# Graph attention on one core: bias of V by VectorE for six tiles of eight, one sum with x moved to GpSimd, one slot's weighing moved to ScalarE, and a new order of work

## The chip, the cores and the metric

The kernel runs on one core of a Trainium2 chip. The metric is the time on the device in microseconds (us), and less is better. The core has TensorE (PE, matrix products into PSUM), VectorE (DVE), ScalarE (ACT), GpSimd (POOL, which here also issues the indirect DMAs), and SyncE (SP, which issues the plain DMAs). Each engine works through its own list of instructions in order. Where one waits, all that stand behind it on that engine wait too.

## The reference

```python
# x (16, 1024, 512), adj (1024, 1024) of zeros and ones, Wq, Wk, Wv (512, 512), 8 heads of 64
h = max(layernorm(x), 0)
q, k, v = h @ Wq + bq, h @ Wk + bk, h @ Wv + bv      # split into heads
scores = q k^T / 8, and -1e9 where adj is 0
out = x + softmax(scores) v                          # per batch, heads side by side
```

The graph is the same for all 16 batches, and each row has few neighbours (the longest lists belong to a few rows).

## The kernel before

**Beginning, once.** The kernel counts each row's neighbours (`degree`), ranks the rows by that number, and lists each row's neighbours (`list_of`). The ranks and the layer norm's factors of batch 0 go through a table in DRAM (`tell`, then `collect`), the lists go through another (`spread`, `collect`). What comes back is a permutation of the rows (`perm_of`) and an index for each gather (`spots`). The rows with the longest lists have what exceeds 11 neighbours cut into pieces of four (`long_rows`, `long_blocks`, `longest`, `count_pieces`, `first_piece`, `owners`, `flip_owners`, `copy_owners`, `list_pieces`, `pieces`, `slots`).

**Each batch.** A batch has eight tiles of 128 rows, in the order 7, 6, 5, 4, 3, 2, 1, 0, so the place `n % 8` of a tile in its batch is 0 for tile 7 and 7 for tile 0. Tile t holds rows with at most `CAPS[t]` neighbours. Per tile:

- `load_x` (GpSimd's indirect DMA), `stats`, `variance`, `power`, `shift` for the layer norm, and `norm` on ScalarE.
- `flip`: four transposes by TensorE; `unflip`: ScalarE copies the result out of PSUM.
- `proj_kv`: K and V, each four fp32 matmuls of 128x512 into one of two PSUM buffers (`pkv`). The bias is a bf16 matmul of 128x512 more (line 1055), or it is left out there and VectorE adds a row of biases while it copies V out of PSUM (line 1073). `bias_by` decides by the table `BIAS_V`. Without it ScalarE copies K or V out (line 1075). This is `evict_kv`; `store_kv` writes both to DRAM.
- `queries`: the same for q, always with the bias by TensorE, into one of two PSUM buffers.

The neighbours' rows of K and V are then fetched in 14 units per batch (`gather`, up to four slots each, six SBUF buffers `g`). Per unit VectorE forms the scores (`multiply`, line 1298; `score`, line 1302), ScalarE the exponent, and each slot's V is weighed: by VectorE in one instruction per slot (`weigh_v`, line 1318), or by ScalarE in eight, one per head (`weigh_s`, line 1332). `by_vector` says how many slots of a unit VectorE takes: `BY_VECTOR` by the unit's size, and one more for the units in `ONE_MORE`. Slots are added (`fold`, line 1337; `join`, line 1344); for tile 0 TensorE does part of that (`add_up`, line 1356; `pass_on` carries a sum of pieces, line 1371). `scale` divides by the sum of weights, `residual` adds x (line 1406; `residual_by_vector` chooses VectorE or GpSimd), `put_out` writes the tile.

K and V of batch b + 1 are projected while batch b's neighbours are weighed. K and V of batch 0 come from the rows as they stand, before the ranking is known (`first` in the names).

**What sets the order.** Every operation has a place, a number in `PLACES`, by batch (the once-only work, `first`, 0, 1, 2, 3 for all in the middle, `next` for the last but one, `last`). `Plan.ordered` sorts each engine's operations by place, and takes at each step the one with the lowest place whose producers and buffers are given. The places are sort keys that were found by a search, not times. The order comes out fixed, engine by engine.

Of the kernel before, what the change touches and what calls it, by code (L numbers as in the profile page):

```python
# [57 lines left out]
UNITS = tuple(unit for t in TILES for unit in PARTS[t])  # L58
# [14 lines left out]
ONE_MORE = ((2, 0),)  # L73
LAST_BY_VECTOR = {(2, 0): 0, (2, 3): 0, (0, 0): 0, (-1, 0): 0, (3, 0): 0, (1, 4): 0}
VECTOR_RESIDUAL = (4,)
# [22 lines left out]
        list_of=(-13.2, -13.4, 13.93, 14.05, -4.33, -7.76, -9.88, 14.25,),  # L98
        tell=(-12.63, -16.97, -13.14, 9.24, 0.89, 16.11, 17.75, 19.88,),
        spread=(45.38, 47.45, 30.7, 45.48, 45.35, 30.46, 22.54, 45.26,),  # L100
        collect=(-9.17, 5.02,),
        others=(14.42,),
        perm_of=(0.42,),
        spots=(26.84,),
        long_rows=(30.4,),
        long_blocks=(16.58, 20.59, 22.61, 24.22, 24.98,),
        longest=(27.18, 29.37, 32.28, 35.43, 36.11, 39.52, 41.52, 44.79, 45.14,),
        count_pieces=(46.89,),
        first_piece=(122.72,),
        owners=(94.07,),  # L110
        flip_owners=(136.43,),
        copy_owners=(113.68,),
        list_pieces=(137.27,),
        pieces=(127.38,),
        slots=(142.24,),
        add_bias=(-19.2, -17.6,),
        spread_bias=(68.07,),
        copy_bias=(89.7,),
# [4 lines left out]
        norm=(75.49, 76.09, 77.09, 77.49, 79.89, 80.09, 80.34, 80.69,),  # L123
        flip=(75.49, 75.69, 76.49, 76.69, 78.69, 78.89, 90.39, 104.64,),
        unflip=(75.89, 76.49, 77.29, 77.89, 80.49, 80.72, 96.22, 97.88,),
        proj_kv=(75.89, 77.49, 76.29, 77.89, 76.89, 78.49, 79.09, 79.29, 86.87, 98.15, 99.79, 107.75, 135.06, 147.6, 153,
            148.32,),
        evict_kv=(76.89, 79.29, 77.69, 79.49, 78.09, 80.29, 80.4, 80.66, 96.1, 96.13, 96.42, 106.28, 154.55, 162.49, 169.71,
            172.46,),
        store_kv=(78.35, 116.17, 119.38, 125.35, 140.7, 146.55, 148.18, 147.06,),  # L130
        variance=(75.89, 76.89, 79.29, 81.69,),
        power=(75.69, 76.29, 78.29, 87.8,),
# [3 lines left out]
        load_x=(30.09, 30.5, 38.8, 45.21, 45.44, 47.92, 49.07, 49.69,),  # L136
        norm=(2.13, 2.31, 24.77, 49.09, 71.39, 77.14, 77.27, 78.66,),
        flip=(50.32, 51.95, 54.11, 55.9, 60.64, 67.45, 67.52, 68.48,),
        unflip=(27.69, 53.06, 72.64, 77.2, 79.54, 81.13, 82.77, 84.23,),
        queries=(67.49, 69.07, 115.56, 126.07, 127.49, 138.29, 148.67, 168.76, 169.97,),  # L140
        gather=(45.09, 65.92, 63.96, 81.66, 82.98, 67.8, 87.05, 86.63, 69.01, 87.14, 102.98, 103.26, 67.61, 108.86, 109.63,
            108.64, 107.92, 79.49, 116.69, 119.1, 130.36, 131.45, 130.44, 102.76, 142.21, 138.67, 142.4, 144.98, 150.63,
            142.37, 142.46, 108, 152.91, 152.09, 152.7, 153.37, 153.1, 152.82, 153.23, 171.08, 171.84, 155.19, 172.79,
            155.41, 171.17, 171.11,),
        multiply=(47.46, 64.59, 81.01, 107.03, 126.74, 113.33, 126.77, 141.63, 149.43, 155.18, 163.45, 170.22, 180.88,
            178.07,),
        score=(47.54, 67.41, 96.06, 111.76, 129.2, 117.87, 128.06, 146.83, 153.31, 155.84, 165.66, 174.39, 181.78, 195.93,),
        exponent=(92.19, 93.82, 105.44, 111.15, 115.51, 115.42, 115.56, 141.97, 143.4, 152.67, 166.31, 172.53, 173.27,
            183.23,),
        row_sums=(64.37, 70.18, 97.04, 118.27, 142.77, 160.52, 163.48, 203.64,),  # L150
        share=(64.49, 74.75, 101.56, 119.16,),
        weigh_v=(69.44, 130.54, 142.01, 144.6, 161.03, 163.57, 170.25, 175.36, 195.82,),
        weigh_s=(92.85, 101.83, 100.44, 95.75, 106.78, 112.94, 106.75, 115.48, 115.39, 115.45, 122.29, 116.89, 121.19, 119.7,
            142.94, 135.53, 142.97, 143.03, 144.58, 154.99, 152.31, 153.27, 163.13, 166.52, 165.91, 171.8, 172.93, 171.74,
            173.08, 173.04, 172.99, 174.92, 175.62, 181.86, 185.22, 185.42, 187.44,),
        fold=(71.91, 97.01, 97.07, 132.47, 137.68, 138.95, 141.69, 143.23, 145.64, 143.05, 153.79, 155.15, 156.82, 161,
            163.76, 171.2, 173.85, 175.66, 181.17, 186.5, 187.92, 183.84, 200, 202.21, 204.35, 204.53,),
        residual=(109.25, 124.53, 138.45, 141.77, 153.19, 171.14, 178.55, 219.35,),
        put_out=(129.95, 130.51, 141.35, 142.43, 153.4, 178.16, 179.5, 225.23,),
        join=(147.89, 161.06, 175.01,),  # L160
        scale=(148.16, 161.67, 176.53, 211.41,),
        copy_q=(145.23,),
        add_up=(188.54, 194.88, 203.87, 205.55,),
        more=(201.41,),
        pass_on=(203.77,),
        seen=(331.72,),
    ),
    1: dict(
        load_x=(-45.57, -43.85, -39.73, -39.1, -35.32, -8.38, 7.1, 14.11,),
        stats=(-63.36, -61.71, -54.75, -49.26, -50.34, -20.16, 1.69, 45.35,),  # L170
        norm=(-12.29, -8.07, -1.29, 11.92, 17.92, 21.28, 45.19, 45.66,),
        flip=(-14.6, 13.76, 33.62, 50.55, 65.56, 72.21, 73.87, 79.53,),
        unflip=(-6.21, -2.22, 15.4, 21.31, 28.65, 37.54, 57.61, 68.73,),
        proj_kv=(17.02, 20.04, 31.75, 42.81, 49.67, 52.6, 71.12, 55.79, 72.24, 74.1, 74.46, 79.5, 79.61, 83.24, 86.3, 90.4,),
        evict_kv=(-2.01, -35.87, 14.8, 20.07, 20.47, 37.41, 38.89, 36.39, 47.71, 60.13, 57.69, 63.79, 70.59, 76.3, 77.5,
            77.55,),
        store_kv=(7.84, 6.03, 7.72, 17.75, 21.65, 22.37, 41.88, 46.5,),
        variance=(-59.83, -48.24, 0.42, 46.54,),
        power=(-31.44, 7.33, 34.59, 50.93,),
        shift=(-56.77, -25.47, 22.23, 52.69,),  # L180
        queries=(92.98, 95.46, 99.76, 113.88, 114.01, 119.61, 134.23, 135.77, 151.42,),
        gather=(53.63, 85.6, 64.02, 85.49, 85.7, 72.03, 102.18, 95.44, 87.81, 104.49, 108.17, 108.68, 107.7, 109.8, 109.4,
            111.58, 112.73, 107.63, 119.79, 126.28, 135.9, 135.96, 135.93, 140.28, 147.73, 148, 149.33, 149.5, 150.8, 150.83,
            149.71, 142.94, 156.83, 157.14, 151.75, 157.7, 150.86, 150.89, 162.73, 165.24, 165.07, 165.98, 165.43, 166.72,
            176.54, 166.09,),
        multiply=(100.67, 106.6, 119.91, 124.46, 149.54, 145.64, 149.6, 154.01, 164.31, 168.95, 171.4, 175.59, 182.84,
            188.66,),
        score=(107.36, 108.32, 124.43, 142.56, 149.57, 145.7, 153.22, 157.27, 165.13, 170.5, 171.68, 182.66, 188.41, 193.53,),
        exponent=(101.25, 100.12, 106.42, 110.23, 116.2, 116.09, 136.58, 137.26, 142.79, 164.86, 172.22, 183.82, 187.9,
            189.8,),  # L190
        row_sums=(111.52, 118.48, 124.49, 145.67, 151.53, 163.54, 171.43, 223.45,),
        share=(112.04, 119.71, 124.55, 145.84,),
        weigh_v=(115.89, 145.87, 155.15, 158.81, 169.44, 171.46, 193.56, 188.61, 193.59,),
        weigh_s=(102.16, 107.3, 103.87, 104.01, 107.98, 108.93, 112.16, 116.05, 121.06, 115.46, 125.94, 135.88, 136.78,
            122.78, 137.3, 139.07, 140.95, 141.59, 137.36, 163.59, 164.34, 153.33, 167.75, 166.89, 171.97, 181.76, 182.84,
            176.37, 187.96, 186.35, 188.1, 189.16, 190.92, 190.49, 191.49, 191.11, 190.86,),
        fold=(119.37, 124.52, 136.3, 135.99, 136.05, 152.83, 147.47, 157.39, 160.24, 157.34, 165.19, 168.14, 169.06, 169.41,
            174.3, 178.51, 174.7, 177.42, 193.62, 193.65, 193.68, 198.47, 195.72, 204.29, 208.27, 212.87,),
        residual=(113.65, 130, 143.43, 153.45, 160.4, 179.56, 185.95, 209.42,),
        put_out=(129.97, 136.02, 156.67, 157.96, 166.22, 183.18, 187.67, 215.86,),  # L200
        join=(163.89, 169.49, 187.98,),
        scale=(164.12, 171.36, 188.49, 227.3,),
        copy_q=(144.08,),
        add_up=(188.22, 192.32, 197.88, 215.67,),
        more=(188.38,),
        pass_on=(191.08,),
        seen=(236.64,),
    ),
    2: dict(
        load_x=(-56.28, -51.47, -39.61, -36, -12.07, 6.83, 6.86, 40.79,),  # L210
# [499 lines left out]
def by_vector(b, B, u):  # L710

    count = UNITS[u][2]
    if b == B - 1:
        return LAST_BY_VECTOR.get(UNITS[u][:2], 1)
# [893 lines left out]
```

## Time and profile before

| | us |
|---|---|
| median of 3 runs (lowest, highest) | 1613.55 (1610.17, 1617.66) |
| the profiled execution: its own time | 1612.02 |
| its span, first to last instruction | 1609.9 |
| PE busy / DVE / ACT / POOL | 1572.1 / 1518.2 / 1444.8 / 1258.7 |
| mean granted TensorE clock | 0.992 of full |
| moved by DMA | 531.56 MB, mean 330 GB/s |

What lies around the span is 1612.02 - 1609.9 = 2.1 us. A busy time is a sum over instructions as the profile shows them; neighbouring instructions overlap a little, so the step from one start to the next is shorter than the duration shown.

### The profile page before, as it was taken

The numbers are of one execution on the slowest core, as the hardware profiler recorded it, in microseconds if no ns is written. First come the engines' busy times: TensorE is split into PE (matmuls) and PEld (weight loads), VectorE is DVE, ScalarE is ACT, GpSimd is POOL, SyncE is SP. The second block draws the span as 40 slices with busy tenths as digits, with TensorE's granted clock in tenths as the row PEclk, the third lists the DMA queues.
The fourth block names the chain that finished last, engine by engine and source line by source line (L and its number), as shares of the span: only waits on it lengthen the run. The fifth ranks groups of instructions, "written<-read, shape, count | busy, mean of one in ns | idle before, by whom it ended". The sixth has DMA issues, their size and how long they took to land. (4 is left out here: it accounts for less than half of the span.)

```text
span 1609.9 us, 19515 instructions
## 1 busy us (share of the span) xinstructions
PE 1572.1 (98%) x4242; PEld 732.0 (45%) x4242; DVE 1518.2 (94%) x2075; ACT 1444.8 (90%) x5428; POOL 1258.7 (78%) x1185
## 2 busy tenths in 40 slices
PE   8999999999999999999999999999999999999687
PEld 4444444444444444444444444444444444444233
DVE  8889999999999999999999999999999999999897
ACT  4459999898999989899898989999998998989897
POOL 3777778887788888888788787878788887786666
PEclk9999999999999999999999999999999999999899
DMA  6499989999999999999999999999999999998886
GB/s 249 141 351 341 334 319 358 329 366 323 341 333 345 366 333 357 325 351 349 339 357 346 345 337 345 344 343 352 330 339 331 341 373 326 338 335 330 324 306 217
DMA packets 149876, 531.56 MB, mean 330 GB/s; under 512 B 19052, under 2 KB 19052, under 8 KB 149752
## 3 DMA queue, kind: packets, MB, share of 16 engines
q0 software_dynamic: 109840, 390.70, 67.9%
q1 hardware_dynamic: 39912, 139.56, 23.0%
q8 instruction: 35, 0.57, 0.1%
q14 instruction: 89, 0.73, 0.1%
HBM read 429.46 MB, written 100.72 MB: 329 GB/s over the span
## 5 line engine op out<-in xcount | busy, mean ns | idle before, releaser
L1332 ACT ACTIVATE g<-g,weights 128x64 f32<-128x64 f32 x4704 | 1160.3, 338 | 40.9 <-DVE weights L1311 37.8
L1288 POOL DMA_INDIRECT g<-kv,index x608 | 642.2, 1056 | 206.7 <-issue 163.2
L1057 PE MATMUL pq<-wq,hT 128*128 128x512 f32 x1024 | 462.4, 595 | 0.0
L1057 PE MATMUL pk<-wk,hT 128*128 128x512 f32 x960 | 431.7, 593 | 0.0
L1057 PE MATMUL pv<-wv,hT 128*128 128x512 f32 x960 | 431.4, 593 | 0.0
L1302 DVE TENSOR_REDUCE weights<-g 128x32 f32<-128x2048 f32 (+2 forms) x224 | 423.7, 1897 | 2.0
L1298 DVE TENSOR_TENSOR g<-g,pq 128x2048 f32<-128x2048 f32 (+2 forms) x208 | 388.7, 1870 | 28.1 <-DMA g<-kv 9.9
L1057 PEld LDWEIGHTS pq<-wq,hT 128*128 128x128 f32 x1024 | 195.8, 191 | 216.9 <-issue 213.2
L1057 PEld LDWEIGHTS pv<-wv,hT 128*128 128x128 f32 x960 | 182.4, 190 | 213.5 <-issue 210.6
L1057 PEld LDWEIGHTS pk<-wk,hT 128*128 128x128 f32 x960 | 182.7, 190 | 201.4 <-issue 196.8
L1337 DVE TENSOR_TENSOR g<-g 128x512 f32<-128x512 f32 (+1 forms) x301 | 253.9, 851 | 9.8 <-ACT g L1332 8.4
L1409 POOL DMA_INDIRECT out_dram<-x,perm x128 | 136.7, 1068 | 39.8 <-issue 30.6
L1002 POOL DMA_INDIRECT x<-in_x_dram,perm x128 | 135.8, 1061 | 34.9 <-issue 32.5
L1337 POOL TENSOR_TENSOR g<-g 128x512 f32<-128x512 f32 x90 | 115.0, 1284 | 17.6 <-DVE g L1337 10.5
L1037 ACT ACTIVATE h<-x,shift,rstd 128x512 f32<-128x512 f32 x120 | 96.5, 807 | 12.0 <-DVE shift L1027 11.4
L1318 DVE TENSOR_TENSOR g<-g,weights 128x512 f32<-128x512 f32 x143 | 101.9, 716 | 1.1 <-ACT weights L1306 0.6
L1356 PE MATMUL acc<-g,ident 128*128 128x512 f32 x170 | 84.4, 612 | 14.6 <-ACT g L1332 10.8
L1044 PEld LDWEIGHTS pht<-ident,h 128*128 128x128 f32 x512 | 63.2, 141 | 68.6 <-issue 52.7
L1406 POOL TENSOR_TENSOR x<-x,o 128x512 f32<-128x512 f32 x64 | 81.9, 1280 | 9.4 <-DVE o L1392 5.0
L1049 ACT COPY hT<-pht 128x512 f32<-128x512 f32 x128 | 73.0, 571 | 16.3 <-PE pht L1044 16.2
L1011 DVE BATCH_NORM_STATS2 st<-x 128x6 f32<-128x512 f32 x120 | 81.2, 677 | 1.6 <-DMA x<-in_x_dram,perm 1.6
L1044 PE MATMUL pht<-ident,h 128*128 128x128 f32 x512 | 76.5, 273 | 3.2 <-ACT hT L1049 1.9
(242 smaller groups left out, 1080.2 us busy)
## 6 DMA issues: line engine op xcount, KB each, us to landing
g<-kv SPq DMA_DIRECT2D x128, 512.0 KB, 7.7
kv<-kvt SPq DMA_DIRECT2D x120, 512.0 KB, 6.9
g<-kv,index POOLq DMA_INDIRECT x608, 6.9
adj<-in_adj_dram SPq DMA_DIRECT2D x8, 512.0 KB, 8.2
x_first<-in_x_dram SPq DMA_DIRECT2D x8, 256.0 KB, 6.0
x<-in_x_dram,perm POOLq DMA_INDIRECT x128, 5.5
out_dram<-x,perm POOLq DMA_INDIRECT x128, 6.6
wk<-in_L_gnn_Wk_dram SPq DMA_DIRECT2D x1, 1024.0 KB
```

What stands on the lines that cost most here:

```text
L1002: nc.gpsimd.indirect_dma_start(out=X[n][:], out_offset=None, in_=x_rows, in_offset=on(ap=perm[:, t : t + 1], axis=0), element_offset=b * N * D
L1037: nc.scalar.activation(HN[n], X[n], AF.Relu, bias=shift, scale=scale)
L1044: nc.tensor.transpose(PH[n][:, c, :], hn[:, ts(c, P)], ident)
L1057: nc.tensor.matmul(pt, HT[n][:, c, :], W[name][:, c, :], start=(apart and c == 0), stop=(n != -NT and c == DC - 1))
L1288: nc.gpsimd.indirect_dma_start(out=G[i][:, s].rearrange("p j d -> p (j d)"), out_offset=None, in_=KV[b % len(KV)][:], in_offset=on(ap=inde ...
L1298: nc.vector.tensor_tensor(k, k, Q[b, t][:, None, :].to_broadcast([P, count, D]), ALU.mult)
L1302: nc.vector.tensor_reduce(weights[:, w, :], heads(G[i][:, :count, 0, :]), AX.X, ALU.add)
L1318: nc.vector.tensor_tensor(v, v, own.to_broadcast([P, n, H, HD]), ALU.mult)
L1332: nc.scalar.activation(v[:, h, :], v[:, h, :], AF.Identity, scale=weights[:, c + s, h : h + 1])
L1337: engine.tensor_tensor(v[:, 0:n], v[:, 0:n], v[:, first : first + n], ALU.add)
L1356: nc.tensor.matmul(ACC[b, home], owner_t if t < 0 else ident, v[:, s, :], start=(u == added_up(b, B, home)[0] and s == 0), stop=(u == adde ...
L1409: nc.gpsimd.indirect_dma_start(out=out_rows[t], out_offset=on(ap=perm[:, t : t + 1], axis=0), in_=X.pop(b * NT + TILES.index(t))[:], in_of ...
```

## The change

The tables that say which engine does what:

```diff
-ONE_MORE = ((2, 0),)
+ONE_MORE = ()
 LAST_BY_VECTOR = {(2, 0): 0, (2, 3): 0, (0, 0): 0, (-1, 0): 0, (3, 0): 0, (1, 4): 0}
-VECTOR_RESIDUAL = (4,)
+NEXT_BY_VECTOR = {}
+VECTOR_RESIDUAL = ()
+NEXT_VECTOR_RESIDUAL = ()
...
-BIAS_V = {0: 'DVE', 2: 'DVE', 4: 'DVE', 6: 'DVE'}
+BIAS_V = {0: 'DVE', 1: 'DVE', 2: 'DVE', 3: 'DVE', 4: 'DVE', 6: 'DVE'}
+LAST_BIAS_V = BIAS_V
...
 def residual_by_vector(b, B, t):
-    return t in (VECTOR_RESIDUAL if b < B - 1 else LAST_VECTOR_RESIDUAL)
+    return t in (LAST_VECTOR_RESIDUAL if b == B - 1 else NEXT_VECTOR_RESIDUAL if b == B - 2 else VECTOR_RESIDUAL)
...
-def bias_by(n, name):
+def bias_by(n, name, B):
+    kinds = LAST_BIAS_V if n >= (B - 1) * NT else BIAS_V
+    return kinds.get(n % NT, "PE") if n >= 0 and name == "v" else "PE"
```

So in each of the 15 batches whose K and V are projected from ranked rows (1 to 15), the tiles at places 1 and 3 lose the bias matmul of V, and their V leaves PSUM through VectorE's addition in place of ScalarE's copy. In batches 0 to 14 the sum of tile 4 with x goes from VectorE to GpSimd, and one slot of the first unit of tile 2, `(2, 0)`, goes from VectorE's one instruction to ScalarE's eight. The last batch's weighing and sums stay as they were.

Every place in `PLACES` from `list_of` on is replaced. Three parts of it, cut to what is spoken of below:

```diff
-        list_of=(-13.2, -13.4, 13.93, 14.05, -4.33, -7.76, -9.88, 14.25,),
+        list_of=(-13.2, -13.4, -4.81, -4.72, -4.29, -5.81, -11.81, -10.72,),
...
-        count_pieces=(46.89,),
-        first_piece=(122.72,),
+        count_pieces=(56.74,),
+        first_piece=(75.94,),
...
-        copy_owners=(113.68,),
+        copy_owners=(170.86,),
...
-        norm=(2.13, 2.31, 24.77, 49.09, 71.39, 77.14, 77.27, 78.66,),
+        norm=(10.32, 13.57, 14.06, 23.48, 49.11, 49.2, 52.33, 56.26,),
```

In the order that comes out, the list of each engine keeps its operations apart from those moved. In the beginning GpSimd stores two tiles of K and V ahead of all the `tell`s, where before it stored one behind the first of them; ScalarE does the norms of batch 0's tiles at places 4 and 5 ahead of the last eviction of `first` K and V, where before the second of them stood behind it; on VectorE `count_pieces` stands behind the first `multiply`, and on TensorE `first_piece` ahead of the queries of tile 5, where before it was the other way round in both. At the end, all engines keep the same operations behind the last projection of K and V, with neighbours swapped here and there.

## The prediction

> **What bounds the kernel now.** I read the page's busy times first, then the slices, then each engine's windows and waits in the middle, then the list of TensorE's instructions in time.
>
> ```profile
> PE 1572.1 (98%) x4242; PEld 732.0 (45%) x4242; DVE 1518.2 (94%) x2075; ACT 1444.8 (90%) x5428; POOL 1258.7 (78%) x1185
> ...
> PE   8999999999999999999999999999999999999687
> ...
> PEclk9999999999999999999999999999999999999899
> ```
>
> TensorE is busy in all slices but the first and the last few. A busy PE need not be PE at its peak, so its windows and its list must confirm it.
>
> ```profile
> 300.00:900.00 600.00, 599.88 (x1621) 280.00 (x1620) 577.71 (x747) 565.09 (x2153) 490.11 (x450) 1.00 0.95 344
> ```
>
> The columns are the window, its length, then busy time of PE, PEld, DVE, ACT and POOL, the granted clock, the DMA share and GB/s. PE is without a gap for 600 us at full clock. Its list shows what a bias costs there:
>
> ```profile
> 827.93 3.60 PE L1057 MATMUL pv<-wv,hT 128*128 128x512 f32 x8
> 831.37 0.60 PE L1044 MATMUL pht<-ident,h 128*128 128x128 f32 x4
> ...
> 835.45 0.38 PE L1055 MATMUL pv<-bias_parts,chosen 128*128 128x512 bf16 x1
> 835.67 3.60 PE L1057 MATMUL pv<-wv,hT 128*128 128x512 f32 x8
> ```
>
> From start to start a projection takes 831.37 - 827.93 = 3.44 us and its bias 0.22 (0.216 over many pairs), though the bias is shown as 0.38. A batch's 24 projections (3.43 each), 20 biases, 8 flips (0.435), 4 additions and one product with the pieces (0.86 each) and `pass_on` (0.14) sum to 94.6 us. The starts of `pass_on` in the list are 94.64 apart (468.77, 563.42, 658.06). So in the middle the time is TensorE's work and nothing else.
>
> At the end it is not. The last projection ends near 1503.5; the last batch's gathers, scores and weighing follow, and TensorE mostly waits:
>
> ```profile
> 1512.91 2.05 PE L1356 MATMUL acc<-g,ident 128*128 128x512 f32 x2 [9.20 <-ACT g L1332]
> ```
>
> **The change, part by part.** The rows by shape (count | busy, mean ns | idle before):
>
> ```profile
> L1332 ACT ACTIVATE g<-g,weights 128x64 f32<-128x64 f32 x4704 | 1160.3, 338 | 40.9 <-DVE weights L1311 37.8 <-DMA g<-kv,index 0.4 <-issue 0.2
> ...
> L1318 DVE TENSOR_TENSOR g<-g,weights 128x512 f32<-128x512 f32 x143 | 101.9, 716 | 1.1 <-ACT weights L1306 0.6
> ...
> L1406 POOL TENSOR_TENSOR x<-x,g 128x512 f32<-128x512 f32 x45 | 58.0, 1289 | 4.7 <-ACT h L1037 1.6 <-issue 1.6
> ...
> L1073 DVE TENSOR_TENSOR kvt<-pv,bias_rows 128x512 f32<-128x512 f32 x60 | 41.0, 683 | 5.2 <-PE pv L1057 5.1
> ...
> L1075 ACT COPY kvt<-pv 128x512 f32<-128x512 f32 x60 | 34.4, 573 | 7.3 <-PE pv L1057 7.0
> ...
> L1055 PE MATMUL pv<-bias_parts,chosen 128*128 128x512 bf16 x60 | 22.8, 379 | 0.0
> ...
> L1406 DVE TENSOR_TENSOR x<-x,g 128x512 f32<-128x512 f32 x16 | 10.7, 666 | 0.0
> ```
>
> *TensorE.* Two biases fewer in each of 15 batches: 30 x 0.216 = 6.5 us, all on the path, so a period of 94.64 - 0.43 = 94.2.
>
> *VectorE.* By steps from start to start: two evictions of V more (0.60 each), one `weigh_v` less (0.60), one sum less (0.58), so 0.02 us more per batch. Nothing in itself, but the period shrinks by 0.43 around it. Its waits over eight periods (468.77 to 1226.15):
>
> ```profile
> DVE g L1298 <- DMA g<-kv: 8.6, 8, 1.7
> DVE g L1298 <- PE pq L1057: 3.2, 5, 0.6
> ...
> DVE g L1298 <- DMA g<-kv,index: 2.0, 2, 1.9
> ```
>
> All its waits there are 22.7 us, 2.84 per batch, of which 0.99 are for TensorE and so real slack; 1.85 are for gathers, ScalarE and GpSimd. Work and contention make 94.67 - 2.84 + 0.02 + 0.05 = 91.90 us (the 0.05 is worked out under GpSimd), which leaves 94.20 - 91.90 = 2.30 for waits that need 1.85. It still fits, barely. I charge 1.0 us in all for places where it doesn't, bounds 0 and 6 (TensorE losing all that it gained).
>
> Behind each new eviction on VectorE stand sums of weights, folds and the next `multiply`, and the next projection but one waits for its PSUM buffer. Summing TensorE's work in the changed order between the end of a projection and the one that reuses its buffer gives 11.4 us of cover for place 1 and 7.3 for place 3. The five VectorE operations ahead of each sum to 6.0 and 5.5 us by their steps, so even with all of them still to do both are covered. The evictions at places 4 and 6, on VectorE already, have 4.1 and 3.65 us (4.9 and 4.1 before). Without cover each costs what it is late.
>
> *ScalarE.* Two copies less (0.47 from start to start), eight heads of one slot more (1.92): 0.98 per batch. Its waits in the same eight periods are 40 us, 5 per batch, so about 3.6 remain: hidden. The first fold of that unit waits for ScalarE's third slot instead of a `weigh_v`; the new order puts it behind the `multiply` and `score` of the first unit of tile 1, where before it stood ahead of both.
>
> *GpSimd.* One sum more, 1.28 per batch at 82% busy, hidden. It follows GpSimd's own last fold of that tile, so it waits for nothing new. Behind it stand three gathers of the second unit of tile 1, each issued in 0.94; `multiply` on VectorE waits for them, and if they come late it is by this 1.28 (the bound of 6 holds a part of that in each batch).
>
> A GpSimd sum and a VectorE sum can hinder each other:
>
> ```profile
> 1499.60 1.29 POOL L1337 TENSOR_TENSOR g<-g 128x512 f32<-128x512 f32 x1
> ```
>
> ```profile
> 1500.01 1.97 DVE L1337 TENSOR_TENSOR g<-g 128x1024 f32<-128x1024 f32 x1
> ```
>
> The same fold takes 1.22 at 854.71; here it lasts until just past its rival, 0.75 longer. Most escape: the means of `weigh_v` (716 against a median of 683) and of the folds (some 15 and 45 above the usual) make about 11 us over the run, against 199 GpSimd sums, so 0.05 each. The Trainium skill, "SBUF — State Buffer", section "Who interferes with whom", speaks against this move: two instructions that both read through the pair of ports that VectorE and GpSimd share don't share time, the second stops until the first ends. By that at its worst VectorE would lose 1.28 us per batch, and the 1.0 us charged above would be 6. I go by the rows.
>
> *Beginning.* The order of TensorE is the same to 60.2 us. Then, before:
>
> ```profile
> 76.56 0.60 PE L1044 MATMUL pht<-ident,h 128*128 128x128 f32 x4
> 79.08 0.66 PE L1044 MATMUL pht<-ident,h 128*128 128x128 f32 x4 [1.91 <-ACT hT L1049]
> ...
> 79.89 5.19 PE L1057 MATMUL pq<-wq,hT 128*128 128x512 f32 x8
> ```
>
> and the window of the same 4 us:
>
> ```profile
> 80.00:84.00 4.00, 4.00 (x7) 1.62 (x6) 3.72 (x14) 1.59 (x3) 3.08 (x4) 0.61 0.88 322
> ```
>
> ScalarE had a norm behind the last eviction of the first K; TensorE waited 1.91 us, the clock fell to 0.61, and a projection took 5.19 for 3.60: with the slower bias 1.75 us lost. Waits of 1.39 (at 10 and 19.7 us) cost no clock. The new order puts that norm ahead of the eviction; the next flip then still waits for an eviction, an unflip and a norm, some 0.9 us. Lead: 1.0, and 1.75 with the clock kept.
>
> Against it, `first_piece` now stands ahead of the third tile's queries and needs `count_pieces`, which stands behind the first `multiply`. That `multiply` began at 96.45, 9.3 us after its first gather was issued (87.15). GpSimd has the same operations ahead of this gather in both orders; three of them took about 0.95 longer than the usual 0.95 before (43.67, 50.96, 55.70), so it is issued between 85.0 and 87.2. TensorE would reach `first_piece` at 97.9 - 2.8 = 95.1 and get it 1.9 us after the `multiply` begins, between 96.2 and 98.4. The lead of 2.8 shrinks by 1.1 to 3.3, and 1.75 more is lost if the clock falls. Another stall of 0.7 us (at 102, for the second `multiply`) falls away, as the queries that met it come later. So between 2.4 us gained and 1.6 lost; I take 1.0 gained, the middle of the two issue times (1.3) less some risk of the clock.
>
> *End.* Both orders have the same ten `weigh_s` on ScalarE and the same additions on VectorE behind the last eviction; GpSimd starts the last batch's gathers when the last `store_kv` has landed. The end moves forward as a whole: 0, bounds 2 gained and 3 lost, by VectorE's waits there (6 us in the last 78).
>
> **Sum.** 1612.0 - 6.5 - 1.0 + 1.0 = 1605.5 for a profiled execution; the profiled one lay 1.5 under the median, so 1607. Its own range is 1603 to 1611.
>
> **Rivals.**
> - *VectorE becomes the bound (slower).* Place: its waits for gathers in each middle batch. Point: waits not for TensorE above 2.30 us per batch. One more late gather per batch like the longest shown (1.9) makes 1.85 + 1.9 = 3.75, a period of 91.90 + 3.75 = 95.65, 1.45 above 94.2, 21.8 over 15 batches in place of the 1.0: 1606 + 21.8 = 1628. For it: DMA is 95% busy, and every place is new. Against: TensorE has no waits in the middle now, and others wait for it.
> - *The gain is mostly eaten.* Those waits come to 2.3 to 2.7, so 0.3 us per batch: 1611 to 1616, no change to be told.
> - *More than the biases.* The beginning gains 2.4, the end 2, and VectorE's term is 0: 1607 - 1.4 - 2 - 1.0 = 1602.6; 1600 to 1603 with a little more at the end.
> - That the change doesn't do what it says is excluded by the order: 30 bias matmuls fewer, 30 VectorE evictions more.
>
> **Numbers.** My forecast 0.60, VectorE as the bound 0.17, mostly eaten 0.18, more gained 0.05. A measurement of this kernel can tell about 0.5%, 8.07 us, from no change: faster is below 1605.5. A little under half of the forecast's chance lies there: 0.29 + 0.05 = 0.34. The rest, 0.31 + 0.18 = 0.49, is the same; slower is 0.17. The range 1600 to 1622 leaves out the slow case and a little of the best.
>
> **What would show it.** Right: `pass_on` starts 94.2 apart, PE without idle from 110 us to the last projection, which ends near 1497; L1055 for pv x30, L1073 x90, L1332 x4824. Right in the beginning: no clock below 1.00 near 80 us, a stall of 1 to 3 us near 95. Wrong: periods above 94.3 with PE waiting for `pkv` or `q` buffers, VectorE's waits for gathers above 2.3 us per batch, or more than 106 us from the last projection to the end.

## The result, and the profile after

The changed kernel takes 1661.29 us (median of 5 runs, 1658.95 to 1661.64) against 1616.53 for the kernel before (5 runs): a ratio of 1.0281, 95% interval 1.0262 to 1.0300. It is 44.8 us slower, and 54 above the forecast of 1607. The profiled execution has a span of 1659.5, 49.6 more than before.

The page first: TensorE's share fell from 98% to 95%.

```profile
PE 1583.9 (95%) x4180; PEld 731.8 (44%) x4212; DVE 1520.8 (92%) x2075; ACT 1463.3 (88%) x5518; POOL 1266.3 (76%) x1200
...
PE   8999999999999999999999999999999999999687
...
PEclk9999999999999999999999999999999999999889
```

The slices look as they did before: a loss of 3% in every slice is still a 9. The windows show it (window, length, busy time of PE, PEld, DVE, ACT, POOL, clock, DMA share, GB/s):

```profile
300.00:900.00 600.00, 582.83 (x1536) 269.54 (x1546) 557.59 (x723) 551.58 (x2101) 471.81 (x441) 0.99 0.91 332
900.00:1000.00 100.00, 97.19 (x255) 44.73 (x257) 91.43 (x118) 91.52 (x351) 75.56 (x73) 0.98 0.91 330
```

Before, PE had 599.88 of these 600 us. Now every engine has less, and the clock is below 1. The starts of `pass_on` are 98.96 apart (784.53, 883.50, 982.46), not 94.20. The waits, over the whole run, name one line (total, times, longest):

```profile
PE pv L1060 <- ACT kvt L1078: 28.1, 11, 3.1
```

Ten of these eleven are one in each of batches 3 to 12, always at the same point. TensorE's list there (start, duration):

```profile
942.57 3.60 PE L1060 MATMUL pv<-wv,hT 128*128 128x512 f32 x8
...
950.53 1.02 PE L1278 MATMUL pq_-1_8022<-q,owner 128*128 128x512 f32 x2
954.25 5.40 PE L1060 MATMUL pv<-wv,hT 128*128 128x512 f32 x8 [2.70 <-ACT kvt L1078]
959.49 0.38 PE L1058 MATMUL pk<-bias_parts,chosen 128*128 128x512 bf16 x1
```

The V projected at 942.57 is that of place 5, which ScalarE copies out; the V at 954.25 is that of place 6 and wants the same PSUM buffer. It starts 2.70 us late, and then takes 5.40 in place of 3.60. Why ScalarE is late stands in ScalarE's list:

```profile
943.80 2.02 ACT L1335 ACTIVATE g<-g,weights 128x64 f32<-128x64 f32 x8
949.04 0.59 ACT L1282 COPY q<-pq 128x512 f32<-128x512 f32 x1 [3.22 <-DVE g L1301]
949.52 2.03 ACT L1335 ACTIVATE g<-g,weights 128x64 f32<-128x64 f32 x8
951.45 0.22 ACT L1309 ACTIVATE weights<-weights 128x32 f32<-128x32 f32 x1
951.70 2.03 ACT L1335 ACTIVATE g<-g,weights 128x64 f32<-128x64 f32 x8
953.63 0.56 ACT L1078 COPY kvt<-pv 128x512 f32<-128x512 f32 x1
```

L1282 is `copy_q`, which copies the queries of tile 0 out of PSUM. It waits 3.22 us for VectorE's first `multiply` of tile 0. In the profile before, `copy_q` (L1279) has no such wait:

```profile
713.97 0.59 ACT L1279 COPY q<-pq 128x512 f32<-128x512 f32 x1
```

VectorE's list of the changed kernel at that point:

```profile
946.73 2.28 DVE L1301 TENSOR_TENSOR g<-g,pq 128x2048 f32<-128x2048 f32 x1
951.58 1.23 DVE L1340 TENSOR_TENSOR g<-g 128x1024 f32<-128x1024 f32 x1 [2.58 <-ACT g L1335]
```

`copy_q` and that `multiply` only read `pq`, so the data ask for no order between them. The built program has a wait between them all the same, in either order (no run here leaves it out): of these two readers of a PSUM tile on two engines, the one written down later waits for the one written down earlier. The instruction of batch 6 in the two builds, before and after (`PE_49` counts TensorE's work, `DVE_49` VectorE's):

```
L1279 TensorCopy q0_6_6153<-pq_6_0_6147 128x512 [waits PE_49]
L1282 TensorCopy q0_6_6300<-pq_6_0_6140 128x512 [waits DVE_49]
```

In the order of before, `copy_q` was written down 7 to 61 operations ahead of that `multiply` (one ahead in batch 15), so it was the `multiply` that had to come behind the copy, which was long done. In the new order `copy_q` comes five operations behind the `multiply` in batches 3 to 12 (and two in 15), and the wait turned round. VectorE then waits in turn for ScalarE's weighing (the 2.58 at 951.58).

The rows that the forecast spoke of, by shape (count | busy, mean ns | idle before):

```profile
L1335 ACT ACTIVATE g<-g,weights 128x64 f32<-128x64 f32 x4824 | 1198.9, 346 | 20.9 <-DVE weights L1314 16.8 <-issue 2.4
...
L1321 DVE TENSOR_TENSOR g<-g,weights 128x512 f32<-128x512 f32 x128 | 99.5, 779 | 0.2 <-ACT weights L1309 0.2
...
L1409 POOL TENSOR_TENSOR x<-x,g 128x512 f32<-128x512 f32 x60 | 76.7, 1279 | 6.8 <-ACT h L1040 2.8 <-issue 1.0 <-DVE g L1340 0.2
...
L1076 DVE TENSOR_TENSOR kvt<-pv,bias_rows 128x512 f32<-128x512 f32 x90 | 61.4, 683 | 21.6 <-PE pv L1060 21.6
...
L1058 PE MATMUL pv<-bias_parts,chosen 128*128 128x512 bf16 x30 | 11.4, 379 | 0.5 <-DVE kvt L1076 0.5
```

The change did what it says. `weigh_v` (L1321) has a mean of 779 ns where it had 716.

The sum of the two spans: 30 biases less, -6.5; nine periods from 487.64 to 1378.86 take 891.2 where 9 x 94.20 would be 847.8, +43.4, less the 1.3 by which before's own nine exceed 9 x 94.64; a tenth wait, at 461.13, +2.8; seven waits between 119 and 304 us of 7.5 in all where before had one of 0.2, +7.3; from the last projection of K and V to the end 107.8 in place of 106.2, +1.6. That is 47.3 of the 49.6.

### The profile page after: what moved, and what is told of

It is laid out like the page before. It is cut to its first block, busy times and chain, and to the rows that moved or that the text cites. A ratio compares the mean times of both kernels' runs of the same rounds, so it can differ in the third digit from the quotient of the medians.

```text
span 1659.5 us, 19557 instructions
## 1 busy us (share of the span) xinstructions
PE 1583.9 (95%) x4180; PEld 731.8 (44%) x4212; DVE 1520.8 (92%) x2075; ACT 1463.3 (88%) x5518; POOL 1266.3 (76%) x1200
## 5 line engine op out<-in xcount | busy, mean ns | idle before, releaser
L1335 ACT ACTIVATE g<-g,weights 128x64 f32<-128x64 f32 x4824 | 1198.9, 346 | 20.9 <-DVE weights L1314 16.8
L1291 POOL DMA_INDIRECT g<-kv,index x608 | 627.9, 1033 | 226.1 <-issue 145.5
L1060 PE MATMUL pv<-wv,hT 128*128 128x512 f32 x960 | 447.9, 611 | 28.1 <-ACT kvt L1078 28.1
L1301 DVE TENSOR_TENSOR g<-g,pq 128x1536 f32<-128x1536 f32 (+2 forms) x208 | 388.3, 1868 | 24.4 <-DMA g<-kv,index 9.9
L1005 POOL DMA_INDIRECT x<-in_x_dram,perm x128 | 137.1, 1071 | 37.5 <-issue 35.7
L1321 DVE TENSOR_TENSOR g<-g,weights 128x512 f32<-128x512 f32 x128 | 99.5, 779 | 0.2 <-ACT weights L1309 0.2
L1409 POOL TENSOR_TENSOR x<-x,g 128x512 f32<-128x512 f32 x60 | 76.7, 1279 | 6.8 <-ACT h L1040 2.8
```

The costliest lines, as they stand in the source:

```text
L1005: nc.gpsimd.indirect_dma_start(out=X[n][:], out_offset=None, in_=x_rows, in_offset=on(ap=perm[:, t : t + 1], axis=0), element_offset=b * N * D
L1060: nc.tensor.matmul(pt, HT[n][:, c, :], W[name][:, c, :], start=(apart and c == 0), stop=(n != -NT and c == DC - 1))
L1291: nc.gpsimd.indirect_dma_start(out=G[i][:, s].rearrange("p j d -> p (j d)"), out_offset=None, in_=KV[b % len(KV)][:], in_offset=on(ap=inde ...
L1301: nc.vector.tensor_tensor(k, k, Q[b, t][:, None, :].to_broadcast([P, count, D]), ALU.mult)
L1321: nc.vector.tensor_tensor(v, v, own.to_broadcast([P, n, H, HD]), ALU.mult)
L1335: nc.scalar.activation(v[:, h, :], v[:, h, :], AF.Identity, scale=weights[:, c + s, h : h + 1])
```

## The experiments

Theory: the turned wait is the loss. Rivals: ScalarE is too full whatever it waits for; VectorE is the bound; or the moves between engines cost more than the 6.5 us. In all edits `order` is the list of operations that the plan gives, in the sequence in which they are written down, and each engine runs its own in that sequence.

**The wait turned back.** Nothing moves on any engine.

```diff
-        for name, *args in plan_of(B):
+        order = plan_of(B)
+        for b in range(B - 1):
+            first, copy = order.index(("multiply", b * NU + 10)), order.index(("copy_q", b))
+            if first < copy:
+                order.insert(copy, order.pop(first))
+        for name, *args in order:
             do[name](*args)
```

> The changed kernel with the list of every engine as it is; only the point at which the first multiply of tile 0 (unit 10) is written down moves, from five operations ahead of copy_q to just behind it, in batches 3 to 12. So VectorE's multiply waits for ScalarE's copy of the same queries, and no longer the copy for the multiply. Theory (the turned wait is the whole loss in the middle): copy_q starts 3.2 us earlier, V of the sixth tile is evicted ahead of TensorE's need, starts of pass_on 94.2 apart in place of 98.96, and 10 x 4.76 = 47.6 us less: about 1614. Rival 1 (ScalarE simply has too much work ahead of that eviction): the projection of V still waits 2 to 3 us for the eviction, 1650 to 1661. Rival 2 (VectorE is the bound, as the prediction's slower case had it): TensorE's wait goes but the period stays near 95.65, so about 1661 - 10 x 3.3 = 1628.

Measured: 1623.81 (before on the same chip 1614.93; ratio 1.0056, 1.0037 to 1.0075). That is 37.5 us less than the changed kernel; 8.9 of the 44.8 us over before are left. So 36 to 37.5 us were this wait, with each engine's list as it was. ScalarE's and TensorE's lists at the same point of a batch:

```profile
834.09 0.58 ACT L1282 COPY q<-pq 128x512 f32<-128x512 f32 x1
834.56 2.04 ACT L1335 ACTIVATE g<-g,weights 128x64 f32<-128x64 f32 x8
836.48 0.24 ACT L1309 ACTIVATE weights<-weights 128x32 f32<-128x32 f32 x1
836.75 2.02 ACT L1335 ACTIVATE g<-g,weights 128x64 f32<-128x64 f32 x8
838.68 0.56 ACT L1078 COPY kvt<-pv 128x512 f32<-128x512 f32 x1
```

```profile
838.39 1.02 PE L1278 MATMUL pq_-1_7204<-q,owner 128*128 128x512 f32 x2
839.29 3.70 PE L1060 MATMUL pv<-wv,hT 128*128 128x512 f32 x8
```

No wait before `copy_q`; the eviction ends at 838.68 + 0.56 = 839.24 and the projection starts at 839.29. In the changed kernel, where it waits, the two are as close (954.19 and 954.25), so the eviction now ends just at the need, with nothing to spare. Quiet periods, those without a longer wait, are 94.3. But ten of the expected 47.6 us didn't come. TensorE waits 8.6 us between 157 and 351 us, and 2.6 us in each of batches 5 and 9, where that same eviction is late again (1.50 at 649.64, 1.48 at 1030.56) and the period slips to 97.4 and 97.3. VectorE has little room left:

```profile
700.00:800.00 100.00, 100.00 (x270) 46.40 (x269) 97.97 (x125) 95.31 (x368) 82.64 (x77) 1.00 0.95 344
800.00:900.00 100.00, 100.00 (x269) 46.42 (x268) 98.99 (x124) 95.29 (x370) 83.58 (x77) 1.00 0.95 345
```

Its busy time was 95.59 and 95.82 in these windows before. The rows by shape over eight periods, first of before, then of this run, show where it went:

```profile
L1337 DVE TENSOR_TENSOR g<-g 128x1024 f32<-128x1024 f32 x48 | 59.2, 1233 | 0.0
L1318 DVE TENSOR_TENSOR g<-g,weights 128x512 f32<-128x512 f32 x71 | 50.4, 712 | 0.4
```

```profile
L1340 DVE TENSOR_TENSOR g<-g 128x1024 f32<-128x1024 f32 x49 | 77.1, 1574 | 0.3
L1321 DVE TENSOR_TENSOR g<-g,weights 128x512 f32<-128x512 f32 x64 | 50.5, 789 | 0.0
```

The long fold (128x1024) takes 0.34 us more (six per batch: 2.0 us), `weigh_v` 0.08 more (eight: 0.6). The single instructions are those that meet a GpSimd sum, VectorE's first, then GpSimd's:

```profile
812.86 1.74 DVE L1321 TENSOR_TENSOR g<-g,weights 128x512 f32<-128x512 f32 x1
...
864.19 2.85 DVE L1340 TENSOR_TENSOR g<-g 128x1024 f32<-128x1024 f32 x1
```

```profile
812.77 1.27 POOL L1409 TENSOR_TENSOR x<-x,g 128x512 f32<-128x512 f32 x1
...
864.67 1.27 POOL L1340 TENSOR_TENSOR g<-g 128x512 f32<-128x512 f32 x1
```

The first is the moved sum of tile 4: the weighing loses 1.06 us to it. The second is a fold of the unit of pieces: VectorE's fold loses 1.63. In the changed kernel the long fold doesn't meet it (its mean is 1223), since it has waited for ScalarE.

The meetings can be counted over the whole run by laying VectorE's weighings, folds and sums beside GpSimd's folds and sums. Before, 16 of VectorE's instructions meet one and lose 7.4 us against their usual times; with the wait turned back 52 do and lose 31.9, though GpSimd has only 15 sums more (214 for 199). The two don't share time: a VectorE instruction that begins while GpSimd's runs ends 0.55 to 0.62 us (128x512) or 1.08 to 1.09 us (128x1024) behind GpSimd's end, in all 40 such meetings of this run. That is most of its usual time (0.68 and 1.22).

**One meeting taken away.** The wait turned back as above, and the fold of the unit of pieces on VectorE:

```diff
+        globals()["POOL_FOLDS"] = tuple(unit for unit in POOL_FOLDS if unit != (-1, 0))
+        for b in range(B - 1):
+            order.remove(("fold", b * NU + 11, 1, 1))
+            order.insert(order.index(("fold", b * NU + 11, 2, 2)) + 1, ("fold", b * NU + 11, 1, 1))
```

> The kernel with the wait turned back (e1_turned, 1623.8), and the last fold of the unit of pieces, (-1, 0), on VectorE instead of GpSimd. In e1_turned GpSimd's fold (864.67, 1.27 us) meets a fold of twice the length on VectorE (864.19), which takes 2.85 in place of 1.22. Theory: VectorE gets 0.68 more and loses 1.63 less, 0.95 per batch better; quiet periods of 94.2 (94.3 before), slips of 1.5 us or less in batches 5 and 9, 3 to 6 us less: 1618 to 1621. Rival (what is left of the loss comes from GpSimd's pauses and from waits for transfers, not from VectorE's work): no change, 1622 to 1626.

Measured: 1619.27 (ratio 1.0031, 1.0019 to 1.0042), 4.5 less than with the wait turned back. The intervals of the two ratios overlap, but the same fold moved in the next pair of runs gives 6.3 less. VectorE does one fold more per batch, and the kernel is faster. The long fold is back near its old mean:

```profile
L1340 DVE TENSOR_TENSOR g<-g 128x1024 f32<-128x1024 f32 x48 | 62.5, 1301 | 0.4 <-ACT g L1335 0.2
```

Over the run VectorE's meetings now cost 18.3 us in place of 31.9. But GpSimd also has 1.28 us less per batch, and this edit doesn't tell the two apart. Quiet periods stayed at 94.3, and one slip of 1.5 us at 649 is left; of the 2.9 us between the two profiled executions, 2.2 lie in nine middle periods (853.9 in place of 856.0), where the slip of batch 9 is nearly gone.

**The sum of tile 4 back on VectorE**, alone, and together with the fold:

```diff
+        globals()["VECTOR_RESIDUAL"] = (4,)
+        for b in range(B - 1):
+            order.remove(("residual", b, 4))
+            order.insert(min(order.index(("weigh_v", b * NU + 5)) + 1, order.index(("put_out", b, 4))), ("residual", b, 4))
```

> The kernel with the wait turned back (e1_turned, 1623.8), and the sum of tile 4 with x on VectorE again, behind the weighing of unit 5. In e1_turned GpSimd's sum of tile 4 (812.77, 1.27 us) meets that weighing on VectorE (812.86), which takes 1.74 in place of 0.68. Theory (what VectorE loses to such meetings keeps it late): VectorE gets 0.58 us of work more and loses 1.06 less, so 0.46 per batch better; the two slips of some 2.7 us in batches 5 and 9 and the waits of batches 1 to 3 shrink, 1 to 4 us less: 1620 to 1623. Rival (the prediction's account, 0.05 us per sum): VectorE is 0.53 worse per batch, with no room left: 2 to 8 us more, 1626 to 1632.

> Both: the wait turned back, the sum of tile 4 and the last fold of the unit of pieces on VectorE. Theory: VectorE is 1.41 us per batch better off than in e1_turned; no slips, quiet periods of 94.2: 5 to 9 us less than e1_turned, 1615 to 1619. Rival (VectorE's work as such is what counts, not the meetings): 1.26 us more per batch on an engine without room, 10 to 15 us more, 1634 to 1639.

Measured: 1639.88 (ratio 1.0142, 1.0118 to 1.0166), 16 more than with the wait turned back, and 1633.54 with both (1.0116, 1.0097 to 1.0135). Neither the 1620 to 1623 nor the 1615 to 1619 of the theory came. The weighing is at 0.68 again, as expected, but a new wait came: GpSimd's next gather wants the buffer that the sum reads, and waits for it.

```profile
815.68 1.28 POOL L1340 TENSOR_TENSOR g<-g 128x512 f32<-128x512 f32 x1
818.68 1.16 POOL L1291 DMA_INDIRECT g<-kv,index  x1 [1.72 <-DVE x L1409]
```

GpSimd's wait of 1.72 is about as long as the sum it no longer does, so it is no better off, and VectorE does 0.6 more. In the run of the sum alone GpSimd's fold of the pieces comes late in ten batches, and TensorE waits for it (first line of its waits from 200 to 1480 us):

```profile
PE acc L1359 <- POOL g L1340: 10.7, 10, 1.7
```

This is the loss in the middle: nine periods take 865.7 us with the sum alone. With both moved they take 854.0, 2.0 less than with the wait turned back, so there VectorE's 1.26 us of added work per batch isn't a loss.

A second part of both losses is not the move at all. In batch 14 the changed kernel's tables leave the sum with GpSimd (`NEXT_VECTOR_RESIDUAL` is empty), and the edit only puts it behind six of GpSimd's gathers. The first of them then waits 7.59 us (1498.20 with the sum alone; 7.58 at 1486.59 with both), VectorE waits for the gather, ScalarE for VectorE, and TensorE waits 5.04 and 4.78 us for `copy_q` (0.34 with the wait turned back). Batch 14 takes 96.9 us in place of 89.3 in both runs. That is 7.6 of the 16 and of the 9.7 us. So these totals don't say what moving the sum back is worth.

**The late eviction put ahead, the turned wait kept.**

```diff
+        for b in range(3, 13):
+            slot = order.index(("weigh_s", b * NU + 9, 1))
+            evict = order.index(("evict_kv", (b + 1) * NT + 5, 1))
+            if slot < evict:
+                order.insert(evict, order.pop(slot))
```

> The changed kernel with the turned wait kept; in batches 3 to 12 ScalarE evicts V of the sixth tile ahead of the eight weighings of unit 9 that stood before it (1.93 us from start to start). Theory (2.70 us of wait, and 1.8 us more because TensorE's clock falls after it): the wait shrinks to 2.70 - 1.93 = 0.77, which is below the waits of 1.39 us that cost no clock in the kernel before, so the projection behind it takes 3.60 and the period is 94.2 + 0.77 = 95.0: 1661 - 10 x 4.0 = 1621. Rival (the long projection has another cause than the wait, the work that runs beside it): it still takes 5.40, only 1.93 per batch is won: 1642.

Measured: 1642.82 (ratio 1.0184, 1.0153 to 1.0214). The total fits the rival's number, the trace doesn't fit its reason:

```profile
942.04 3.70 PE L1060 MATMUL pv<-wv,hT 128*128 128x512 f32 x8 [0.63 <-ACT kvt L1078]
945.58 0.38 PE L1058 MATMUL pk<-bias_parts,chosen 128*128 128x512 bf16 x1
945.79 3.60 PE L1060 MATMUL pk<-wk,hT 128*128 128x512 f32 x8
950.72 0.38 PE L1058 MATMUL pv<-bias_parts,chosen 128*128 128x512 bf16 x1 [1.33 <-DVE kvt L1076]
```

The wait is 0.63 and the projection 3.70, so the 1.8 us did come with the long wait. What ate the rest is the wait of 1.33 at 950.72: VectorE still stands 2.57 us before a fold (941.43) whose slot is weighed behind the late `copy_q`, and 0.59 before another (948.84) whose slot is weighed behind the eviction put ahead. Its eviction of place 6 comes right behind, at 949.98.

**Parts of the change in the old order.** The two biases alone:

```diff
+        order = plan_of(B)
+        BIAS_V.update({1: "DVE", 3: "DVE"})
```

> The kernel before with one part of the change alone: in batches 1 to 15 the bias of V of the tiles at places 1 and 3 is added by VectorE, at the point of the order at which ScalarE copied these V before; nothing else moves. The prediction's term: 30 x 0.216 = 6.5 us less on TensorE, period 94.2, so 0.4% below the kernel before. Rival 1 (VectorE has no room for 1.2 us more per batch without the sum and the weighing that the change takes from it: 91.88 us of work in 94.64, waits of 1.85 needed): the period stays at 94.64 or rises by up to 1 us, so 0 to 15 us slower. Rival 2 (an eviction that comes late on VectorE stalls a projection as ScalarE's did in the changed kernel): a wait for kvt on TensorE in each batch, and 15 x 1 to 5 us slower.

Measured: 1621.22 (10 runs; ratio 1.0038, 1.0024 to 1.0052): 6.3 more, not 6.5 less. Quiet periods are 94.2, as the sum had it; others are 94.5 to 98.3, with many waits below 1.2 us, and one of 2.56 for VectorE's eviction (1476.03). So TensorE's saving shows where nothing waits, and waits elsewhere cost more than it.

All three moves, with the sum behind GpSimd's own fold of tile 4:

```diff
+        order = plan_of(B)
+        BIAS_V.update({1: "DVE", 3: "DVE"})
+        globals().update(ONE_MORE=(), VECTOR_RESIDUAL=())
+        for b in range(B - 1):
+            order[order.index(("weigh_v", b * NU + 6))] = ("weigh_s", b * NU + 6, 2)
+            order.remove(("residual", b, 4))
+            order.insert(order.index(("fold", b * NU + 3, 1, 1)) + 1, ("residual", b, 4))
```

> The kernel before with all three moves of the change between engines (bias of V at places 1 and 3 by VectorE, sum of tile 4 by GpSimd, one slot of the third tile by ScalarE), each at the point of the old order at which the work stood, the sum just behind GpSimd's own fold of that tile; no new places. Theory (the loss is in the new order, not in the moves): VectorE has its old sum of work, so the gain of 6.5 us shows at least in part: 1608 to 1613, and no period of 98.96. Rival 1 (VectorE has no room for the two evictions whatever is taken from it, as bias alone gave 6.3 us more): 1617 to 1622. Rival 2 (GpSimd's added sum meets VectorE's work here too and costs up to 1.27 per batch): 1620 to 1630.

Measured: 1631.65 (ratio 1.0102, 1.0084 to 1.0120). The number lies just above rival 2's, and the reason isn't rival 2's: no operation of VectorE is longer (the long fold 1210 ns), but VectorE waits for the slot that ScalarE now weighs, up to 2.2 us at a time (its waits over eight periods; 2.2 us in all before):

```profile
DVE g L1337 <- ACT g L1332: 19.6, 16, 2.2
```

So at the old places the moves lose too. Whether an order exists in which they gain, no run shows.

**TensorE's saving by itself.** The bias of V at places 1 and 3 left out by all:

```diff
-            apart = n == -NT or bias_by(n, name) != "PE"
+            apart = n == -NT or bias_by(n, name) != "PE" or (name == "v" and n >= 0 and n % NT in (1, 3))
```

> The kernel before, in which TensorE leaves out the bias of V at places 1 and 3 in batches 1 to 15 and nobody adds it (ScalarE copies these V as before): this part of the output is missing. So TensorE has the saving of the change, 30 x 0.216 us, and no other engine has any more work. Theory (the saving is real, the price is paid on the other engines): 6.5 us less than the kernel before, periods of 94.2: 1608. Rival (the engines beside TensorE hold the period at 94.64 already: VectorE has 2.8 us of waits per batch and GpSimd 3.2): 0 to 2 us less, 1612 to 1615.

Measured: 1609.89 against 1613.95 (10 runs; ratio 0.9973, 0.9963 to 0.9983): 4.1 of the 6.5 us, even where nobody pays. The interval (2.7 to 6.0 us) leaves out both the theory's 6.5 and the rival's 0 to 2. Of nine middle periods four are 94.2 to 94.3, the others 94.6 to 95.

**More of it.** The bias of K left out (for `"k"` and `n >= 0` in the same line), and then also TensorE adding the bias of V at places 2 and 6 again:

> The kernel before without the bias of K in batches 1 to 15. Over one row's neighbours it adds the same number to every score, so the softmax doesn't change. 120 x 0.216 = 25.9 us less on TensorE, nothing more anywhere. If TensorE stayed the bound: periods of 92.9 and 1589. Theory (what VectorE does besides waiting for TensorE is 91.83 plus 1.85 of waits for others, so 93.7): periods near 93.7, 14 us less, 1600. Rival (VectorE and GpSimd without room slip from batch to batch, as in the runs with the wait turned back): 1606 to 1614.

> As the run before it without the bias of K, and TensorE adds the bias of V at places 2 and 6 again, whose V ScalarE copies: per batch TensorE has 8 biases fewer and 2 more (1.30 us less than the kernel before), VectorE 1.20 less, ScalarE 0.94 more. The opposite of the change: work goes from VectorE to TensorE. Theory: TensorE stays the bound with periods of 94.64 - 1.30 = 93.34, so 15 x 1.30 = 19.5 us less, 1595, as VectorE needs 90.6 + 1.85 = 92.5. Rival 1 (ScalarE, with 4.7 us of waits per batch, comes late with its two evictions more, as it did in the changed kernel): 1605 to 1620. Rival 2 (GpSimd's list, 91.5 of 94.64 us without a wait, is next and slips): 1598 to 1605.

Measured: 1604.44 (ratio 0.9943, 0.9920 to 0.9966), below both kernels with nothing of the result left out, and 1618.63 (1.0036, 1.0025 to 1.0048). Of 25.9 us on TensorE 9.5 came through: of nine middle periods two are 93.4, six 94.2 to 94.7, one 95.7. In the second TensorE waits for ScalarE's evictions of K and norms (3.6 us each from 200 to 1480 us), and 6.4 us for evictions between 139 and 178, as its rival 1 said, though the time lies at that rival's upper end.

Last, in the kernel without K's bias one fold per batch left to TensorE (dropped from `order` and from `folds`), GpSimd's of unit 11 or VectorE's of unit 13:

> The kernel before without the bias of K (n2_no_k_bias, 1604.4), and in batches 0 to 14 GpSimd's last fold of the unit of pieces is left to TensorE, which adds two slots of that unit in place of one (0.86 us more on TensorE, 1.28 less on GpSimd per batch). In n2_no_k_bias most periods were 94.3 with TensorE's work at 92.9 and GpSimd without a wait over 0.36 us through whole batches. Theory (GpSimd's list is what comes next behind TensorE): periods fall to TensorE's 92.9 + 0.86 = 93.8, some 0.5 us in each of 12 batches, 1597 to 1600. Rival (VectorE is next): no change or slower by the slips that TensorE's new work brings, 1603 to 1608.

> As the run before it, but what is left to TensorE is VectorE's last fold of the last unit of tile 0: 0.86 us more on TensorE, 0.60 less on VectorE, nothing less on GpSimd. Theory (GpSimd's list is next): periods stay near 94.3, 1603 to 1606. Rival (VectorE is next): periods fall to 93.8, 1597 to 1600.

Measured on a chip where the kernel before took 1622.25: 1617.70 (ratio 0.9964, 0.9949 to 0.9979) and 1613.42 (0.9940, 0.9922 to 0.9957). Neither gained on the 0.9943 without the fold's move. With VectorE eased four periods fell to 93.9, with GpSimd eased none fell below 94.1, and nine middle periods take 848.6 and 853.6 us. That speaks for VectorE; but with neither eased they took 848.9, and the whole didn't gain, so which engine comes next behind TensorE stays open.

## Why the prediction was wrong

**The step that failed: the cover behind an eviction.** The prediction summed TensorE's work between a projection and the one that reuses its buffer for evictions on VectorE, and judged ScalarE by its average ("about 3.6 remain: hidden"). The eviction that stalls TensorE is ScalarE's, of V at place 5. Its cover, TensorE's work between the two projections, is 5.4 us (946.0 to 951.4), and even with the wait turned back it ends just at the need (839.24, start at 839.29). So a `copy_q` that is 3.2 us late goes almost whole to TensorE, which waits 2.70 in each of batches 3 to 12. And it read the new order engine by engine, which can't show the turned wait: that depends on the sequence across engines, and stood in the waits of the built program.

**Size.** TensorE starts 2.86 us later than it would (the wait of 2.70, and 0.16 by which one matmul's start otherwise overlaps the end of the one before), and the projection takes 1.80 more at the slow clock: 4.66. The quiet work was 94.3, so 98.96, as measured. The prediction knew from 80 us of before that a wait of 1.91 had cost 1.75 more, but used it for the beginning only.

**TensorE's term, -6.5.** Right in the middle: quiet periods of 94.2 with the biases alone, 94.3 with the wait turned back. But it isn't all on the path: alone it gave 4.1.

**VectorE's term, +1.0, bounds 0 to 6.** Too small. The 0.05 us per GpSimd sum was the price of the old order, where few of them meet VectorE (7.4 us over 199 sums). With the wait turned back 214 sums cost 31.9, 0.15 each; in the batch shown the moved sum costs 1.06 and the fold of the pieces 1.63. The prediction's own pair showed what a meeting is: VectorE's fold ended at 1501.98, 1.09 us behind its rival's end at 1500.89, not "just past" it. Here the rule that the prediction set aside was nearer: the Trainium skill, "SBUF — State Buffer", section "Who interferes with whom", has one of two such instructions wait for the other's end. That fits the 40 meetings above. It also has the one that issues first go first; the fold of the pieces doesn't show that by the starts in the trace, as VectorE's began at 864.19, 0.48 us ahead of GpSimd's, and still ended 1.09 behind it. And 1.28 us per batch against 0.45 of room (2.30 less 1.85) would have made some 12 us over 15 batches, not the 6 that the prediction put there. How much of the kernel's time the meetings are is less sure: the run with one fewer gave 4.5 us, with GpSimd eased too.

**GpSimd, "hidden".** Its busy share of 82% leaves out a pause of some 0.3 us around most of its DMAs; in its list all pauses longer than 0.35 us sum to 0 to 3.2 us per batch over seven periods of before, and to 0 to 0.5 over four quiet ones with the wait turned back (2.2 in those of batches 5 and 9). A sum of 1.28 was much of its room.

**Beginning and end.** No cold clock near 80 us (wait 1.01 at 79.18) and 1.27 at `first_piece` (98.51, within the 1 to 3 forecast), as worked out; 1.19 at 88.76 was not. But the prediction's account of the beginning ended at 102 us, and the new order has 7.5 us of waits between 119 and 304. The end lost 1.6 where 0 was taken.

**The rivals.** None reached the 1661. "VectorE becomes the bound" gave 1628 and named gathers; VectorE's meetings were part of what was left with the wait turned back (1623.8), late gathers in each batch weren't.

## What to carry to other kernels

When an order is changed, list the waits that the program itself gains or loses, across engines: two readers of one PSUM tile can be put one behind the other, and which of them waits is set by the sequence in which they are written down. Work out the cover of every eviction on every engine, not only of those that the change moves, and price a wait of TensorE with the slow stretch that can follow it. Where VectorE and GpSimd both work on rows in SBUF, count which instructions meet in the new order, and don't carry over the old order's mean. An engine's room is its unexplained pauses, not 100% less its busy share; here, where VectorE had 2.8 us of waits in a period of 94.6 and GpSimd up to some 3, a saving on TensorE came through only in part.

## What the runs showed of the hardware

**VectorE and GpSimd.** VectorE's instructions that read two SBUF operands (weighing, fold, sum) and GpSimd's sums ran one behind the other, whichever came first. Where VectorE's was held, it ended 0.55 to 0.62 or 1.08 to 1.09 us behind GpSimd's, as said. Where GpSimd's was held, it took up to 2.19 us in place of 1.27 and ended 1.13 behind VectorE's.

**The clock.** In the changed kernel the first wait of 2.70 us (461.13) was followed by a projection of 3.70 at a clock of 1.00 (461 to 465), the next nine by one of 5.40 (0.62 at 558 to 562, 0.61 at 954 to 958). With the fold moved back, waits of 1.34 (89.23) and 1.75 (99.44) were followed by 0.60 (99 to 103); with the wait turned back, 1.14 and 0.78 at the same points by 1.00, and so was one of 2.90 at 304.13, where the changed kernel's 2.99 (303.50) was followed by 0.64. So the length of one wait doesn't decide alone. The Trainium skill, "TensorE: Matmul & The Clock Gate", section "What's actually happening", tells of windows of about 3.4 us that run on freely, which would make it a matter of where the wait falls; no run here shows the windows.

**GpSimd's DMA issues.** In GpSimd's list over eight periods of the kernel before, the indirect DMAs that run beside a VectorE sum, fold or weighing for over 0.3 us take 1.20 us in the mean (43% over 1.2), the others 0.98 (hardly any over 1.2); with the wait turned back 1.23 against 0.98. VectorE's instruction isn't longer for it (1.21 for the long fold at 806.87, beside an issue of 1.75 at 807.15).
